# Layer 0 of a four-layer graph network: row steps ordered behind the value checks, constants made in steps over the first loads, six checks moved to layer 2

## The chip, the cores and the metric

The kernel runs on one core of a Trainium2 chip. The metric is device time in microseconds. The engines named below are PE (matrix multiplication), DVE (VectorE), ACT (ScalarE), POOL (GpSimd) and SP, whose queue issues the large loads from HBM.

## The reference

`x` is 4096 rows of 64 features, `adj` a 4096 x 4096 matrix of zeros and ones in float32 (64 MiB). Four layers follow each other, each `x = layernorm(x + layer(x, adj))`. All four read the whole of `adj`.

```python
# layer 0
deg = jnp.clip(jnp.sum(adj, axis=1, keepdims=True) + 1.0, 1.0, None)
h_neigh = (adj @ X + X) / deg
z = jnp.concatenate([X, h_neigh], axis=1) @ W + b
out = jax.nn.relu(z)
out = out / jnp.maximum(jnp.linalg.norm(out, axis=1, keepdims=True), 1e-12)
# layers 1 and 3: hyperbolic attention over the edges
adj_att = sigmoid(left[:, None] + right[None, :] + b_att) * adj
support_t = einsum('ij,ijd->id', adj_att, logmap(x[:, None], x[None, :], c))
out = proj(expmap(x, support_t, c), c)
# layer 2: the last 100 neighbours, weights halving with each step back
w = mask * where(pos > 0, 0.5 ** (k - pos), 0.0)
out = w @ (x @ weight) + bias
```

## The kernel before

`adj` is transposed on its way in and read four times, once in each layer. A layer works through four **groups** of 1024 output rows. `GROUPS` holds them in the order s = 3, 2, 1, 0; the text numbers them in the order of work, group 0 (s = 3) to group 3 (s = 0). Each group goes through 16 **loads** `g` = 15 down to 0. A load is one tile `edges`, 128 partitions by two blocks of 1024 columns in float32, 1.0486 MB, issued on SP's queue (L708). There are six buffers for such tiles; a buffer comes free when all that reads the tile is done.

In **layer 0** each load is used by eight matmuls (L1561, 128x512 each), which add up `adj @ X` in three bfloat16 parts together with the degree. Some loads are also used by a **check** (L871): a DVE instruction over the whole tile that counts the values other than 0 and 1, since the fast path assumes them. A check is done once for each of the 64 tiles of `adj` in the whole run: `checked_later(s, g)` says whether it is done in layer 0 or put off to layer 2, which reads the same tiles again. Before the change, eight loads of each group are checked in layer 0 (g = 4, 6, 8, 10 and 12 to 15) and eight in layer 2.

The **row work** of a group (the end of a layer for its 1024 rows, and the preparation of the next layer) is written as generators. `later` puts one into a queue. `tick` is called four times for each load in layer 0; it advances a place counter and runs the generators that are due, so a generator's `yield n` means "go on n ticks later", and its instructions are emitted between those of the loads. `mark` separates the instructions emitted by loads ("pairs") from those emitted by row steps. Where `anchored[0]` is set, it gives every row instruction on PE, ACT and DVE an order dependence on the last pair instruction of the same engine that was emitted ahead of it. Before the change `anchored[0]` is set only in the attention layers.

In layer 0 and layer 2, PE and ACT execute in the order of emission (`tc.manual_schedule(engines=FIXED)`). DVE and POOL do not: there a planner orders the instructions by its own estimate of when their inputs are ready, within the dependences.

The row work of a group in layer 0 is `end_0` (it starts in the first tick of the next group, with the matmuls L1510 and L1511), then `norm_rows` and `prepare`. `prepare` puts its second half, `second`, into the queue 44 ticks later: DVE's L975 to L1008, among them L994, L997 and L987, three copies on ACT (L971 to L973), small copies on POOL (L979 to L984), four sets of transposes on PE (L1023) with ACT's copies after them (L1027), and the attention scores. `linear` makes `x @ W` of the group's own rows (PE L1370 and L1381, DVE L1496). `constants` spreads the small parameters over the partitions (L1472, copied out at L1473), derives the curvature values (`curved`) and turns the two attention vectors into columns (`att_columns`, products at L855). The products and the spreading share one PSUM tile, `aux`.

`move` ends an attention layer for one group. Group 3's `move` of layer 1 and `supports`, which turns its rows into layer 2's operand, run inside layer 2's first pass, `wide_pass`, which works on groups 0 and 1 together (matmuls L1743 and L1755). There ACT's L1302 (tanh) and L1394 (the rows in half precision) stand at fixed places between the exponentials L1750.

Of the kernel before, what the change touches and what calls it, by code (L numbers as in the profile page):

```python
# [21 lines left out]
D = 64  # L22
# [39 lines left out]
def gnn_stack_kernel(  # L62
# [509 lines left out]
    def stream(fits):  # L572

        with ExitStack() as st:
# [57 lines left out]
            def later(steps, second=False, wait=0):  # L632
                queues[int(second)].append([steps, place[1] + wait])

            def in_turn(tag, *parts):
                for part in parts:
                    yield from (part or ())
                done.add(tag)
# [47 lines left out]
            def spare_ends():  # L686
                while held:
                    tick(1)
                spare.clear()
# [21 lines left out]

            def checked_later(s, g):

                return g in (0, 1, 2, 3, 5, 7, 9, 11)

            def grp(name, bufs=None):
                kw = {"bufs": bufs} if bufs else {}
# [129 lines left out]
                nc.scalar.dma_start(t, src[:, :, None, :].to_broadcast([1, 2, 2, D]))  # L847
                return t

            def att_columns(rows_of, name):  # L850


                t = aux.tile([P, 2], F32, name="aux")
                for u in range(2):
                    nc.tensor.matmul(  # L855
                        t[:, u : u + 1], rows_of[:, u].rearrange("p k d -> p (k d)"),
                        one_row[:, :1], start=True, stop=True,
                    )
                w = row.tile([P, 2], F32, name="att_w")
                V.tensor_copy(w, t)  # L860
                parts = keep.tile([P, 7], BF16, name=name)
                for k in range(3):
                    of = parts[:, k : k + 4 : 3]
                    V.tensor_copy(of, w)
                    V.tensor_sub(w, w, of)
                V.memset(parts[:, 6:], 1.0)
                return parts
# [7 lines left out]
            def curved(c, name, least):  # L875


                c2, sc, rsc, of_y, root, short, by_root, by_short = (
                    num(keep, name + n, 1)
                    for n in (  # L880
                        "_c2", "_sc", "_rsc", "_of_y", "_root", "_short", "_by_root", "_by_short",
                    )
                )
                V.tensor_scalar(c2, c, -2.0, None, ALU.mult)
                V.tensor_copy(rsc, rsqrt(c, "rsc"))
                V.tensor_mul(root, rsc, c)
                V.tensor_copy(by_root, rsc)
                V.tensor_scalar(by_short, rsc, 1.0 / least, None, ALU.mult)
                V.tensor_scalar(of_y, rsc, -((2.0 * UNIT) ** -0.5), None, ALU.mult)
                V.tensor_scalar(rsc, rsc, 0.996, None, ALU.mult)  # L890
                V.tensor_scalar(sc, root, -((2.0 * UNIT) ** 0.5), None, ALU.mult)
                V.tensor_scalar(short, root, least, None, ALU.mult)
                return c, c2, sc, rsc, of_y, root, short, by_root, by_short
# [551 lines left out]
            with ExitStack() as lp:  # L1445
# [23 lines left out]
                def constants():  # L1469

                    t = aux.tile([P, 2 * D + 3], F32, name="aux")
                    nc.tensor.matmul(t, one_row, given, start=True, stop=True)  # L1472
                    V.tensor_copy(given_b, t)  # L1473
                    V.tensor_mul(c1, r_sb, r_sb)
                    V.reciprocal(c1, c1)
                    V.memset(c3, 1.0)
                    V.tensor_copy(ident16, ident)
                    V.memset(sum_w[:, D:], 0.0)
                    V.tensor_copy(sum_w[D:, :D], w0_sb[D:, :])
                    V.memset(count_w, 0.0)  # L1480
                    V.memset(count_w[D:, D:], 1.0)
                    V.tensor_copy(count_w[:D, :D], sum_w[:D, :D])
                    return (
                        curved(c1, "k1", 1e-15**0.5), curved(c3, "k3", 1e-15),
                        att_columns(att_rows1, "att1"), att_columns(att_rows3, "att3"),
                    )

                V.memset(third[:, :, D : D + 1], 1.0)
                parts_of(GROUPS[0])
# [8 lines left out]
                def end_0(s, tops):  # L1498
# [43 lines left out]
                        1, s, att1, batt1_sb, curve1, 1e-15, good[:, 0], 70  # L1542
                    )

                with tc.manual_schedule(engines=FIXED):
                    for s in GROUPS:
                        sums = [ps.tile([P, W], F32, name="acc") for _ in range(2)]
                        counts = [ps.tile([P, W], F32, name="acc") for _ in range(2)]
                        parts = ((first, sums, P), (third, counts, D + 1))
                        for g in reversed(range(NB // 2)):  # L1550
# [22 lines left out]
                                                start=False, stop=False,  # L1573
                                            )
                            if s == GROUPS[0] and g == NB // 2 - 3:
                                curve1, curve3, att1, att3 = constants()
                                nc.scalar.dma_start(w2_sb, w2)
                                nc.scalar.dma_start(w2_twice[:D], w2)
                                nc.scalar.dma_start(w2_twice[D:], w2)
                                later(in_turn((0, s), linear(0, s, w0_sb[:D, :], own_part)))  # L1580
                            tick(4)
                        need((0, s))
                        tops = []
                        for h in range(2):
                            top = row.tile([P, W], F32, name="sums", bufs=2)
# [13 lines left out]
                            later(in_turn((0, s - 1), own_of))  # L1599

                spare_ends()


            place[0] = 1
# [285 lines left out]
```

## Time and profile before

| | us |
|---|---|
| median of three runs | 1066.32 (1062.9 to 1067.3) |
| the profiled execution's own time | 1064.98 |
| its span, first to last instruction | 1063.3 |
| PE busy | 985.4 (93%) |
| DVE busy | 901.2 (85%) |
| ACT busy | 753.4 (71%) |
| POOL busy | 339.1 (32%) |
| bytes moved | 271.62 MB, mean 255 GB/s |

Layer 0's matmuls run from 7.2 to 183 us of the span, layer 1's from 186 to 518, layer 2's first pass from 514 to 610. A busy PE is not PE at its peak, since matmuls are pipelined and their ends are modelled. In the lists of instructions the columns are start, duration, engine, line, operation, output from input, shapes and count, and in brackets the idle time of the engine ahead of it with what ended it. In the groups the columns are the count, busy time and mean duration in nanoseconds, and the idle time ahead. A wait of the DMA queue (SPq) names the engine and line that freed the buffer, with total time, count and longest.

### The profile page before, as it was taken

The page shows a single profiled execution, that of the slowest core. Times are in us where ns is not written, and L with a number is a line of the kernel's source. Part 1 is how long each engine was busy: PE and PEld are TensorE (multiplying, and loading weights), DVE is VectorE, ACT ScalarE, POOL GpSimd, SP SyncE. Part 2 cuts the span into 40 slices and gives each one's busy share as a digit, 9 for nine tenths or more (in the row PEclk, how much of TensorE's full clock was granted, in tenths as well). Part 3 has the DMA queues.
Part 4 walks back from the last instruction along what each step waited for, and adds up shares of the span by engine and source line. Part 5 has one row for each costly group of instructions (what it writes and reads, how often), then busy time and mean ns, then how long its engine had stood idle before and what let it go on. Part 6 is the DMA issues. An engine that isn't in the chain of part 4 may idle for free.

```text
span 1063.3 us, 13594 instructions
## 1 busy us (share of the span) xinstructions
PE 985.4 (93%) x4845; PEld 400.7 (38%) x4845; DVE 901.2 (85%) x1383; ACT 753.4 (71%) x876; POOL 339.1 (32%) x695
## 2 busy tenths in 40 slices
PE   4998998879999999999999999997999999999991
PEld 2454554323333333333333344442333333333330
DVE  6677878779999999999485579857899999999996
ACT  0013122859989888888677688896998888888970
POOL 0011222470064464455200020105401562573670
PEclk8999999989999999999999999998999999999996
DMA  8999999836665656566599999994465766665600
GB/s 338 369 420 367 389 390 387 336 107 222 216 220 198 238 204 232 198 224 219 218 331 341 372 357 314 322 328 179 163 240 194 245 226 209 237 218 198 228 3 22
DMA packets 38580, 271.62 MB, mean 255 GB/s; under 512 B 4710, under 2 KB 4710, under 8 KB 5734
## 3 DMA queue, kind: packets, MB, share of 16 engines
q1 hardware_dynamic: 37728, 270.03, 69.7%
q8 instruction: 40, 0.66, 0.2%
q10 hardware_dynamic: 774, 0.63, 0.2%
q14 instruction: 38, 0.31, 0.1%
HBM read 269.58 MB, written 1.05 MB: 255 GB/s over the span
## 4 chain that ended last, share of the span: by engine, by line
PE 66%; DVE 18%; POOL 5%; DMA 4%; ACT 4%; issue 2%; ACTq 0%; SPq 0%; POOLq 0%; DVEq 0%
PE acc L1121 18%; PE z L1743 11%; PE z L1143 8%; PE z L1149 8%; PE z L1146 7%; DVE t L1170 5%; DVE t L1167 5%; PE acc L1561 4%; DMA edges<-in_adj_dram 3%; PE z L1755 3%; DVE junk L871 2%; PE z L1709 2%; ACT sq L1750 1%; ACT sq L1164 1%; POOL sq L1525 1%
## 5 line engine op out<-in xcount | busy, mean ns | idle before, releaser
L1167 DVE SCALAR_TENSOR_TENSOR t<-z,sig 128x1024 f32<-128x1024 f32 x256 | 309.1, 1218 | 22.4 <-ACT sq L1164 19.8
L1164 ACT ACTIVATE sq<-z 128x1024 f32<-128x1024 f32 x256 | 255.4, 1022 | 62.1 <-PE z L1149 31.7
L1170 DVE SCALAR_TENSOR_TENSOR t<-sq,t 128x2048 f32<-128x2048 f32 x127 | 293.4, 2311 | 0.3
L1161 ACT ACTIVATE sig<-left_b,right 128x1024 f32<-128x1024 f32 x256 | 287.3, 1150 | 6.5 <-DVE t L1167 6.0
L1121 PE MATMUL acc<-t,xe 128*64 128x512 f32 x1024 | 261.5, 616 | 13.4 <-DVE t L1170 13.4
L1143 PE MATMUL z<-edges,two_i 128*128 128x512 bf16 x512 | 200.3, 391 | 6.2 <-DVE t L1167 6.2
L1149 PE MATMUL z<-dst,src 74*128 74x512 f16 x512 | 194.8, 380 | 0.0
L1146 PE MATMUL z<-lo_hi,hi_lo 128*128 128x512 f16 x512 | 193.7, 378 | 0.0
L1750 ACT ACTIVATE sq<-z 128x512 bf16<-128x512 f32 (+1 forms) x192 | 137.9, 741 | 39.5 <-PE z L1743 38.8
L1121 PEld LDWEIGHTS acc<-t,xe 128*64 128x64 f32 x1024 | 64.9, 138 | 144.4 <-issue 110.0
L871 DVE SCALAR_TENSOR_TENSOR t<-edges 128x2048 bf16<-128x2048 f32 x32 | 74.4, 2335 | 28.7 <-DMA edges<-in_adj_dram 28.6
L1561 PE MATMUL acc<-edges,first 128*128 128x512 bf16 x256 | 81.1, 398 | 18.1 <-DMA edges<-in_adj_dram 17.9
L1143 PEld LDWEIGHTS <-two_i 128*128 128x128 bf16 x512 | 50.3, 98 | 118.7 <-issue 73.1
L1743 PE MATMUL z<-edges,pass_by 128*128 128x512 bf16 x248 | 86.4, 388 | 6.3 <-ACT sq L1750 5.8
L1743 PE MATMUL z<-edges,enter 128*128 128x512 bf16 x256 | 88.2, 387 | 0.0
L871 DVE SCALAR_TENSOR_TENSOR junk<-edges 128x2048 bf16<-128x2048 f32 x32 | 73.1, 2284 | 14.9 <-DMA edges<-in_adj_dram 14.9
L1561 PE MATMUL acc<-edges,third 128*65 128x512 bf16 x256 | 80.5, 396 | 0.0
L1149 PEld LDWEIGHTS <-src 74*128 74x128 f16 x512 | 49.1, 96 | 73.5 <-issue 11.9
L1146 PEld LDWEIGHTS <-hi_lo 128*128 128x128 f16 x512 | 50.2, 98 | 63.7 <-issue 18.3
L1270 POOL TENSOR_TENSOR w_att<-x,u 128x512 f32<-128x512 f32 x6 | 18.2, 3028 | 169.9 <-ACT u L1264 169.9
L1709 PE MATMUL z<-sq,halves 128*128 128x512 bf16 x128 | 48.1, 377 | 0.6 <-ACT sq L1750 0.6
L1525 POOL TENSOR_TENSOR sq<-z 128x512 f32<-128x512 f32 x4 | 10.1, 2526 | 117.2 <-DVE z L1523 97.4
(466 smaller groups left out, 996.5 us busy)
## 6 DMA issues: line engine op xcount, KB each, us to landing
edges<-in_adj_dram SPq DMA_DIRECT2D x256, 1024.0 KB, 4.9
x<-in_x_dram SPq DMA_DIRECT2D x4, 256.0 KB
out_dram<-x ACTq DMA_DIRECT2D x2, 256.0 KB
out_dram<-x SPq DMA_DIRECT2D x2, 256.0 KB
w_sb<-in_L_gnn_W_dram ACTq DMA_DIRECT2D x1, 32.0 KB, 4.9
w_twice<-in_L_gnn_weight_dram ACTq DMA_DIRECT2D x2, 16.0 KB, 8.7
given<-in_L_gnn_b_dram ACTq DMA_DIRECT2D x1, 0.2 KB
given<-in_L_gnn_bias_dram ACTq DMA_DIRECT2D x1, 0.2 KB
```

Of the source, the lines that this page charges most:

```text
L871: V.scalar_tensor_tensor(junk, a, 0.0, a, ALU.not_equal, ALU.not_equal, accum_out=odd[:, n : n + 1])
L1121: it = nc.tensor.matmul(acc[h * D : (h + 1) * D, :], xe[:, j, :], t[:, k, h * W : (h + 1) * W], start=j == BLOCKS[0], stop=j == BLOCKS[-1],)
L1143: nc.tensor.matmul(half, two_i, edge[:, at : at + W], start=True, stop=False)
L1146: nc.tensor.matmul(half, hi_lo[:, of], lo_hi[:, to], start=False, stop=False)
L1149: last = nc.tensor.matmul(half, src[:, of], dst[:, to], start=False, stop=True)
L1161: nc.scalar.activation(sig, left_b, AF.Sigmoid, bias=right[:, j : j + 1])
L1164: nc.scalar.activation(sq[:, k], zp, AF.Square, bias=ROOT + OFF, scale=-1.0 / UNIT)
L1167: V.scalar_tensor_tensor(ts[k][:, k], zp, 0.0, sig, ALU.max, ALU.mult)
L1170: V.scalar_tensor_tensor(t, sq, HIGH**2, t, ALU.add, ALU.mult)
L1561: nc.tensor.matmul(accs[h][:m], lhs[:, j, :], edge[:, at : at + W], start=j == BLOCKS[0], stop=j == BLOCKS[-1],)
L1743: nc.tensor.matmul(z[:, h : h + W], lhs, rhs[:, h : h + W], start=j == BLOCKS[0], stop=True, skip_group_check=True,)
L1750: weighed[0] = nc.scalar.activation(w, z[:, :n], AF.Exp, bias=-(OFF_EDGE + CUT) * LN2, scale=-LN2)
```

## The change

- `checked_later`: in group 0 all loads with g under 12 are checked in layer 2; in group 1 also g = 4 and 6.
- `att_columns` is split: the products become `att_products`.
- `constants` becomes a generator with pauses of 4, 8, 8, 8 and 4 ticks, run in the queue ahead of the group's `linear`, where it had been emitted whole behind load g = 13. Its results are taken from the list `made` at the end of the group.
- `anchored[0]` is set in layer 0 for every group but the first, and cleared behind `spare_ends()`.

```diff
             def checked_later(s, g):

-                return g in (0, 1, 2, 3, 5, 7, 9, 11)
+                if s == GROUPS[0]:
+                    return g < 12
+                return g in (0, 1, 2, 3, 5, 7, 9, 11) or (s == GROUPS[1] and g in (4, 6))
...
-            def att_columns(rows_of, name):
-
+            def att_products(rows_of):
 
                 t = aux.tile([P, 2], F32, name="aux")
...
+                return t
+
+            def att_columns(t, name):
+
                 w = row.tile([P, 2], F32, name="att_w")
...
                     nc.tensor.matmul(t, one_row, given, start=True, stop=True)
+                    yield 4
                     V.tensor_copy(given_b, t)
+                    yield 8
                     V.tensor_mul(c1, r_sb, r_sb)
...
-                    return (
-                        curved(c1, "k1", 1e-15**0.5), curved(c3, "k3", 1e-15),
-                        att_columns(att_rows1, "att1"), att_columns(att_rows3, "att3"),
-                    )
+                    made.append(curved(c1, "k1", 1e-15**0.5))
+                    made.append(curved(c3, "k3", 1e-15))
+                    for rows_of, name in ((att_rows1, "att1"), (att_rows3, "att3")):
+                        w = att_products(rows_of)
+                        yield 8
+                        made.append(att_columns(w, name))
+                    yield 4
...
                     for s in GROUPS:
+                        anchored[0] = s != GROUPS[0]
...
                             if s == GROUPS[0] and g == NB // 2 - 3:
-                                curve1, curve3, att1, att3 = constants()
                                 nc.scalar.dma_start(w2_sb, w2)
                                 nc.scalar.dma_start(w2_twice[:D], w2)
                                 nc.scalar.dma_start(w2_twice[D:], w2)
-                                later(in_turn((0, s), linear(0, s, w0_sb[:D, :], own_part)))
+                                own_of = linear(0, s, w0_sb[:D, :], own_part)
+                                later(in_turn((0, s), constants(), own_of))
                             tick(4)
                         need((0, s))
+                        curve1, curve3, att1, att3 = made
...
                 spare_ends()
+                anchored[0] = False
```

## The prediction

> **What bounds the kernel now.** The change sits in layer 0 and in the first pass of layer 2, so I read those two stretches and not the shares of the whole span. First the page's groups: what one load of 128x2048 edge values costs on each engine.
>
> ```profile
> L871 DVE SCALAR_TENSOR_TENSOR junk<-edges 128x2048 bf16<-128x2048 f32 x32 | 73.1, 2284 | 14.9 <-DMA edges<-in_adj_dram 14.9
> L1561 PE MATMUL acc<-edges,first 128*128 128x512 bf16 x256 | 81.1, 398 | 18.1 <-DMA edges<-in_adj_dram 17.9
> ```
>
> A check costs VectorE 2.28 us. In the chain of waits, PE takes 1.8 us for the eight matmuls of a load. Then the DMA view of the first 230 us (slices of 5.75 us):
>
> ```profile
> GB/s 205 278 408 410 422 259 372 388 416 429 425 416 425 413 311 309 390 429 416 422 419 396 298 292 409 423 423 420 420 409 298 403 407 427 389 215 261 151 218 54
> ```
>
> Six slices in a row (46 to 80 us) average 421 GB/s: a load of 1.0486 MB then takes 2.49 us, more than PE's 1.8. So transfer is the floor, and the holes are the dips near 30, 83, 130 and 175 us. Table by stage:
>
> ```profile
> 17.00:31.00 14.00, 8.16 (x41) 5.03 (x39) 12.07 (x50) 0.58 (x1) 0.00 (x0) 0.65 0.97 396
> 57.20:99.60 42.40, 38.74 (x225) 21.72 (x224) 33.30 (x85) 7.79 (x12) 8.82 (x9) 1.00 0.96 385
> 99.60:143.50 43.90, 41.31 (x242) 23.51 (x241) 34.59 (x99) 10.55 (x17) 8.74 (x9) 0.96 0.96 383
> ```
>
> The first row holds the start, the others are groups 1 and 2 (counted in order of work from 0). Last columns: granted clock, DMA share, GB/s. The share says 0.96, the bytes say 383 of 421. Who holds the loads back is in the DMA queue's own waits, here for 0 to 47 us (first line) and 91 to 135 us (the other two):
>
> ```profile
> SPq L708 <- PE acc L1561: 19.3, 8, 7.5
> ...
> SPq L708 <- DVE junk L871: 31.1, 8, 6.0
> SPq L708 <- PE acc L1561: 5.5, 4, 2.7
> ```
>
> Early it is PE's matmuls, later the checks. PE's timeline has the early cause:
>
> ```profile
> 18.18 0.49 PE L1472 MATMUL aux<-given,one_row 1*128 1x131 f32 x2
> 23.71 1.01 PE L855 MATMUL aux<-one_row,xw 1*128 1x1 f32 x4 [5.04 <-DVE given_b L1473]
> ...
> 27.35 1.06 PE L1561 MATMUL acc<-edges,first 128*128 128x512 bf16 x2
> ```
>
> PE stands from 18.7 to 27.35 us in the constants: their products reuse one PSUM bank, which VectorE empties only at 23.4, behind two checks. Load g=12 had landed before 21.2 (its check ran then). The six edge buffers fill; no load is issued from 22 to 31 us. The later cause is in VectorE's timeline of group 2:
>
> ```profile
> 129.58 0.64 DVE L994 TENSOR_TENSOR xw<-x,g 128x512 f32<-128x512 f32 x1
> ...
> 131.32 0.68 DVE L997 TENSOR_TENSOR xe<-xw,m 128x512 f32<-128x512 f32 x1
> 131.92 2.29 DVE L871 SCALAR_TENSOR_TENSOR junk<-edges 128x2048 bf16<-128x2048 f32 x1
> ...
> 134.13 0.69 DVE L987 TENSOR_TENSOR ys<-y,ys 128x512 f16<-128x512 f32 x1
> ...
> 136.58 2.28 DVE L871 SCALAR_TENSOR_TENSOR junk<-edges 128x2048 bf16<-128x2048 f32 x1
> ```
>
> The two checks are g=6 and g=4. L994, L997 and L987 belong to `second`, which the program emits 44 steps (11 loads) after `prepare`, behind check g=4; the scheduler hoisted them.
>
> **What the Trainium skill says.** "VectorE: DVE Perf Modes", the perf-mode tier table: a two-input fp32 operation has only the 1x rate; for N=2048 it gives 2293 ns. The trace has 2284 ns, so a check can't be cheapened, only moved. "DMA: Bandwidth & Descriptors", Bandwidth: 425 GB/s for a 16 MB transfer; the 421 sustained here agrees. "Perfetto Trace Analysis", Identifying the Most-Contended Engine: occupancy of the 16 DMA engines misleads, use bytes; here 0.96 busy beside 383 GB/s agrees. "TensorE: Matmul & The Clock Gate", Part 1: after an idle window of about 3.4 us PE falls to half clock; after the 5 us wait the table has 0.65, and the next eight matmuls took 3.41 us instead of 1.81.
>
> **The change, part by part.** Six checks leave layer 0: g=4, 6, 8, 10 of group 0, g=4 and 6 of group 1; 6 x 2.28 = 13.7 us of VectorE go to layer 2. The instructions of the constants stay the same; PE gets them at g=13, g=10 and g=8, after which group 0's own linear part ends at g=0 instead of g=8. From group 1 on each row step on VectorE gets an order dependence on the last check emitted ahead of it; PE and ACT were in program order already.
>
> *Transfer floor.* By 28.75 us 9.91 MB were moved, 1.05 of it x: 8.45 loads. From there at 2.49 us each, load n lands at 28.75 + (n-8.45) x 2.49: load 17 at 50.0, 33 at 89.9, 64 at 167.1.
>
> *Group 0.* Without the stall PE takes g=12 at 18.7. Loads g=7 and g=6 are then released by their buffers' checks (ends 21.1 and 23.4, where they are now), the rest by PE alone. Transfer stays full. The copy to `given_b` (23.4) is there before PE reaches g=10's products (24.5): no new wait. PE ends load 17 at 50.0 + 1.8 = 51.8; before 57.2: **-5.4**.
>
> *Group 1.* Checks g=6 and 4 are gone. Check g=8 ended at 83.5; I shift it by the 5.4 to 78.1. Load 30 reuses its buffer and lands 4.9 us later (the page's median), 83.0 against a floor of 82.4: 0.6 lost. Load 33 lands at 90.5, PE ends it at 92.3; before 99.6: **-7.3**.
>
> *Group 2.* Check g=8 now ends at 127.4 - 7.3 = 120.1; load 46 lands at 125.0, against 122.9: 2.1 lost. Check g=6 loses the pieces of `second` hoisted ahead of it, 1.8 us (the small ones, L994 and L997): 134.2 - 7.3 - 1.8 = 125.1; load 48 lands at 130.0, where it is anyway. Load 49 at 132.5, done at 134.3; before 143.5: **-9.2**.
>
> *Group 3.* Check g=8 at 159.8, g=6 at 176.2 - 9.2 - 2.4 = 164.6; loads 62 and 64 could land at 164.7 and 169.5, the floor from 132.5 has 164.9 and 169.9. PE's last matmul ends near 172.2 (0.5 for the transposes ahead of it); before 183.0: **-10.8**. At the pure floor it would be -13.6.
>
> *The new wait.* `second` now stands behind check g=4. Behind it on VectorE is only the next group's check; PE's transposes L1023 wait for its L987, and load g=0's matmuls queue behind them. POOL's small copies of `second` (4.7 us, ended at 135.4 and 176.8) move along; only the third and fourth transposes need them, 6 us later in PE's order, and POOL is otherwise empty there. The three weight DMAs on ACT's queue stay at g=13. In group 2 check g=4 would end at 127.4, L987 some 3 us on at 130.4; PE arrives at 129.3, and load 48 lands at 130.0: 0 to 1 us, inside the 10.8, of which I keep **10.5**. After layer 0 comes a chain of POOL row steps and layer 1's pairs, bound by PE and VectorE (DMA share 0.62 from 290 to 515): the gain passes through.
>
> *Layer 2.* PE runs without a gap from 518 to 610 us, so only a delay that reaches PE counts. Checks don't hold loads there: load g=5 landed at 568.1 and PE releases it at 580.8, while its checks took until 573.2. What they can delay is the row chain of the last `move`, through ACT's fixed order:
>
> ```profile
> 542.14 0.23 DVE L1296 TENSOR_SCALAR un<-un,k_short 128x8 f32<-128x8 f32 x1
> ...
> 545.50 0.20 ACT L1302 ACTIVATE th<-un 128x8 f32<-128x8 f32 x1
> ...
> 560.72 0.69 DVE L1360 TENSOR_TENSOR x<-z,y 128x512 f32<-128x512 f32 x1
> ...
> 567.07 0.61 ACT L1394 CAST x_hl<-x 128x512 f16<-128x512 f32 x1
> ```
>
> The slack is 3.1 us ahead of L1302 and 5.7 ahead of L1394. Checks g=10 and g=8 (one each) fall into the chain: 2.3 and 4.6 us, within both. The pairs at g=6 and g=4 fit VectorE's gaps at 563.6 (4.5 us) and 573.2 (6.5 us in two). If check g=6 comes ahead of L1360 or a check waits for its load in front of the chain, some us come through. Bounds 0 and 9: if the whole chain stood behind the checks of g=6 (landed near 562, done at 566.7), its last 9 us would end near 576 instead of before 567. I take **1**. A gain is excluded: PE is full.
>
> Sum: -10.5 + 1 = -9.5. The profiled execution has a span of 1063.3 and a time of 1065.0; the median shown is 1066.3, 1.3 above. 1065.0 - 9.5 + 1.3 = 1056.8, say **1057**.
>
> **The rivals.**
> *Only the stall counts.* Order on VectorE may yield nothing: the norm steps, which legitimately follow check g=15, delay checks as before. For: most of the row work ahead of check g=8 is of that kind. Against: the hoisted pieces are seen. The early dips (slices 6 and 7) hold (421-259 + 421-372) x 5.75 / 421 = 2.9 us, and the missing checks of group 1 some 3: -3 to -6, 1060 to 1063.
> *The transposes become the wait (slower).* Place: L1023 behind L987 behind check g=4, in groups 2 and 3. Point: my 130.4 against PE's 129.3 and the load's 130.0, so it decides as soon as check g=4 is over 1 us later than I put it. Price: each further us once per group; with check g=4 ending where it ended and the 5 us of hoisted steps plus a check behind it, 7 us each: -7.3 + 14 = +6.7, 1073. For: the margin is thin. Against: the check itself moves up by the same pieces.
> *Layer 2 takes it back.* The chain behind all checks to g=6: +9 - 10.5 = -1.5, 1065.
> *It doesn't do what it says.* The scheduler may have other orders at the same cost, transfer stays at 385 GB/s: 1066.
>
> **Numbers.** About 0.5% (5.3 us) is what a measurement of this kernel can tell from no change. Forecast 0.62 (1052 to 1062), stall only 0.16 (half of it faster by over 0.5%), transposes 0.11, layer 2 0.06, nothing 0.05. Faster 0.70, same 0.18, slower 0.12. The range 1051 to 1064 leaves out the slower rival and the upper end of the last two.
>
> **What would show it.** PE with no wait over 1 us between 18 and 28 us and a clock of 1.0 there; GB/s near 421 from 12 to 80 us; group 1 begun near 52 us; VectorE with L994, L997 and L987 after check g=4 in groups 2 and 3; layer 0's last matmul near 172. In layer 2 PE without gaps, L1394 not waiting. A PE wait at L1023 over 2 us, or PE waiting on ACT near 545 or 567, would prove me wrong, as would layer 0 ending after 178.

## The result, and the profile after

| | us |
|---|---|
| before, median of 13 runs | 1066.32 |
| after, median of 13 runs | 1062.86 (1059.22 to 1070.47) |
| ratio after to before | 0.9965, 95% interval 0.9946 to 0.9984 |
| the profiled execution of after | 1065.97, span 1064.2 |

The change is worth 3.5 us; 9.5 were forecast. Executions of one kernel lie over 10 us apart, and the profiled one of after is 3.1 above its median, so what two profiles differ in is only taken for the change here where further profiles show it too.

Layer 0 first: the table by stage of after, with the start and groups 1 and 2 as in the prediction (the last three columns are granted clock, DMA share and GB/s), and then the DMA view of the first 230 us.

```profile
17.00:31.00 14.00, 10.50 (x52) 4.97 (x51) 12.65 (x55) 0.00 (x0) 0.00 (x0) 0.88 1.00 402
55.46:97.40 41.94, 38.29 (x221) 21.73 (x224) 29.08 (x76) 7.77 (x12) 6.75 (x9) 1.00 0.99 400
97.40:139.20 41.80, 39.32 (x237) 22.72 (x240) 35.33 (x99) 10.44 (x18) 6.75 (x9) 1.00 0.98 393
```

```profile
GB/s 195 302 400 373 427 416 423 416 427 417 422 417 426 373 315 423 420 425 413 427 390 311 349 427 426 423 415 416 355 388 426 426 376 262 219 214 164 241 187 0
```

The start moves 402 GB/s where it moved 396, with PE at clock 0.88 for 0.65; the hole near 30 us (259 before) is gone. The holes near 83, 123 and 165 us are still there. PE's timeline at the start:

```profile
17.86 0.49 PE L1477 MATMUL aux<-given,one_row 1*128 1x131 f32 x2
18.28 0.62 PE L1573 MATMUL acc<-edges,first 128*128 128x512 bf16 x2
...
25.65 1.01 PE L1573 MATMUL acc<-edges,first 128*128 128x512 bf16 x2 [3.25 <-DMA edges<-in_adj_dram]
```

The stall in the constants (L1477 is the old L1472) is gone, but PE now waits for a load, and falls to half clock again (1.01 us for a pair of matmuls, 0.61 at full clock). In the later groups the order on VectorE is as written: `second` (L992, L999, L1002) stands behind check g = 4 of group 2.

```profile
128.81 2.29 DVE L876 SCALAR_TENSOR_TENSOR junk<-edges 128x2048 bf16<-128x2048 f32 x1
...
131.10 0.68 DVE L992 TENSOR_TENSOR ys<-y,ys 128x512 f16<-128x512 f32 x1
132.06 0.68 DVE L999 TENSOR_TENSOR xw<-x,g 128x512 f32<-128x512 f32 x1
132.78 0.69 DVE L1002 TENSOR_TENSOR xe<-xw,m 128x512 f32<-128x512 f32 x1
```

Layer 0's end comes 4.4 us earlier ("deg 3" in the table of the experiments). Then two things eat it. The first is PE's clock at the handover to layer 1 (before: 1.00 all through):

```profile
178.00:182.00 4.00, 2.73 (x24) 2.31 (x22) 1.01 (x4) 3.98 (x7) 0.00 (x0) 1.00 1.01 422
182.00:186.00 4.00, 4.00 (x18) 2.95 (x18) 0.09 (x1) 3.15 (x4) 0.00 (x0) 0.58 1.02 426
186.00:190.00 4.00, 3.77 (x20) 2.66 (x21) 2.50 (x5) 0.36 (x1) 0.16 (x1) 0.57 0.97 360
```

The second is in layer 2's first pass. There the last group's rows `x` (VectorE, L1365) are split into two half-precision parts `x_hl`: a cast on ACT (L1399), then a subtraction on POOL (L1400), then PE's transposes (L1405). VectorE's timeline of after, and then ACT's, POOL's and PE's:

```profile
566.38 0.69 DVE L1365 TENSOR_TENSOR x<-z,y 128x512 f32<-128x512 f32 x1
566.98 2.28 DVE L876 SCALAR_TENSOR_TENSOR t<-edges 128x2048 bf16<-128x2048 f32 x1
...
569.19 3.23 DVE L876 SCALAR_TENSOR_TENSOR t<-edges 128x2048 bf16<-128x2048 f32 x1
```

```profile
567.15 0.62 ACT L1399 CAST x_hl<-x 128x512 f16<-128x512 f32 x1 [1.95 <-DVE x L1365]
```

```profile
567.84 2.43 POOL L1400 TENSOR_TENSOR x_hl<-x,x_hl 128x512 f16<-128x512 f32 x1 [25.37 <-ACT x_hl L1399]
```

```profile
570.33 0.62 PE L1405 MATMUL aux<-ident,x_hl 128*128 128x128 f16 x8 [3.36 <-POOL x_hl L1400]
```

The same place in before, POOL and VectorE:

```profile
543.30 1.16 POOL L1395 TENSOR_TENSOR x_hl<-x,x_hl 128x512 f16<-128x512 f32 x1 [30.22 <-ACT x_hl L1394]
567.76 1.16 POOL L1395 TENSOR_TENSOR x_hl<-x,x_hl 128x512 f16<-128x512 f32 x1 [23.30 <-ACT x_hl L1394]
```

```profile
543.35 3.26 DVE L871 SCALAR_TENSOR_TENSOR t<-edges 128x2048 bf16<-128x2048 f32 x1 [0.84 <-DMA edges<-in_adj_dram]
...
568.15 2.91 DVE L871 SCALAR_TENSOR_TENSOR t<-edges 128x2048 bf16<-128x2048 f32 x1 [4.54 <-DMA edges<-in_adj_dram]
```

Two things are to be read. First, in after ACT waits 1.95 us for `x`, and PE 3.36 us behind it; before, neither waited. Second, durations: POOL's subtraction takes 1.16 us or 2.43, a check 2.28 or 3.26. The one that is under way runs on at its usual pace; the other stands until it is done, which shows as a long instruction and not as a wait. In before POOL started 0.05 us ahead of the check at 543 and 0.39 ahead at 568; in after a check was already running. A check has two inputs in SBUF (the same tile twice). The Trainium skill, "SBUF — State Buffer", Who interferes with whom, states that a VectorE instruction with two SBUF inputs contends with a GpSimd instruction that reads SBUF, and that the order of issue decides which of the two is blocked. The durations agree (543.30 + 1.16 is 1.1 after the check's start, which is 0.98 longer than usual). The prediction priced the check on VectorE alone and not whom it locks out.

### The profile page after: what moved, and what is told of

It is laid out like the page before. It is cut to its first block, busy times and chain, and to the rows that moved or that the text cites. A ratio compares the mean times of both kernels' runs of the same rounds, so it can differ in the third digit from the quotient of the medians.

```text
span 1064.2 us, 13506 instructions
## 1 busy us (share of the span) xinstructions
PE 979.2 (92%) x4760; PEld 400.3 (38%) x4845; DVE 904.9 (85%) x1383; ACT 753.0 (71%) x876; POOL 327.6 (31%) x695
## 4 chain that ended last, share of the span: by engine, by line
PE 58%; DVE 23%; DMA 7%; POOL 4%; ACT 4%; issue 3%; ACTq 0%; SPq 0%; POOLq 0%; DVEq 0%
PE acc L1126 17%; PE z L1757 8%; PE z L1151 8%; PE z L1148 7%; PE z L1154 7%; DVE t L1172 6%; DVE t L1175 6%; DMA edges<-in_adj_dram 6%; DVE junk L876 3%; PE acc L1573 3%; PE z L1723 2%; PE z L1769 2%; ACT sq L1169 1%; ACT sq L1764 1%; DVE t L876 1%
## 5 line engine op out<-in xcount | busy, mean ns | idle before, releaser
L1148 PE MATMUL z<-edges,two_i 128*128 128x512 bf16 x463 | 182.7, 395 | 5.4 <-DVE t L1172 5.4
L876 DVE SCALAR_TENSOR_TENSOR t<-edges 128x2048 bf16<-128x2048 f32 x38 | 87.3, 2310 | 20.9 <-DMA edges<-in_adj_dram 20.7
L1573 PE MATMUL acc<-edges,first 128*128 128x512 bf16 x241 | 77.0, 396 | 21.9 <-DMA edges<-in_adj_dram 21.2
L1757 PE MATMUL z<-edges,enter 128*128 128x512 bf16 x248 | 85.9, 387 | 0.4
L876 DVE SCALAR_TENSOR_TENSOR junk<-edges 128x2048 bf16<-128x2048 f32 x26 | 59.4, 2285 | 11.7 <-DMA edges<-in_adj_dram 11.6
L1723 PE MATMUL z<-sq,halves 128*128 128x512 bf16 x122 | 45.9, 377 | 0.8 <-ACT sq L1764 0.6
L1380 ACT COPY x_t<-aux 64x512 f32<-64x512 f32 x8 | 4.6, 576 | 58.3 <-PE aux L1375 58.3
```

The source lines that it names most:

```text
L876: V.scalar_tensor_tensor(junk, a, 0.0, a, ALU.not_equal, ALU.not_equal, accum_out=odd[:, n : n + 1])
L1148: nc.tensor.matmul(half, two_i, edge[:, at : at + W], start=True, stop=False)
L1573: nc.tensor.matmul(accs[h][:m], lhs[:, j, :], edge[:, at : at + W], start=j == BLOCKS[0], stop=j == BLOCKS[-1],)
L1757: nc.tensor.matmul(z[:, h : h + W], lhs, rhs[:, h : h + W], start=j == BLOCKS[0], stop=True, skip_group_check=True,)
```

## The experiments

All profiles in one table. "deg" is the start of the first reciprocal in each group's end (L1516 before, L1526 after), 1.93 us behind PE's first matmul of that end in groups 0 to 2, 2.0 to 2.3 in group 3. "Gap" is the time from group 3's first to its second reciprocal: 4.06 at PE's full clock. "Pass" is layer 2's first pass, between the copies of the sums that end layer 1 and the pass. The subtractions are POOL's first and second `x_hl` in layer 2 (v: on VectorE). Ratios are to before, with 95% interval.

| kernel | deg 0 | deg 1 | deg 2 | deg 3 | gap | pass | subtractions | ratio |
|---|---|---|---|---|---|---|---|---|
| before | 59.14 | 101.53 | 145.40 | 185.41 | 4.06 | 92.94 | 1.16, 1.16 | |
| after | 57.39 | 99.36 | 141.14 | 180.99 | 6.13 | 96.27 | 1.15, 2.43 | 0.9965 (0.9946 to 0.9984) |
| e1 after again | 56.29 | 97.00 | 139.00 | 179.57 | 6.42 | 97.23 | 1.15, 2.43 | 0.9964 (0.9949 to 0.9979) |
| e2 checks alone | 59.75 | 101.61 | 144.93 | 184.97 | 4.07 | 97.22 | 1.15, 2.42 | 1.0024 (1.0007 to 1.0041) |
| e3 constants alone | 55.78 | 98.21 | 141.74 | 185.53 | 5.71 | 96.34 | 3.18, 1.16 | 0.9989 (0.9969 to 1.0009) |
| e4 order alone | 59.43 | 100.74 | 141.61 | 181.45 | 6.93 | 96.35 | 3.19, 1.15 | 0.9979 (0.9959 to 0.9999) |
| e5 constants, order | 56.05 | 96.79 | 137.62 | 177.44 | 4.07 | 96.36 | 3.20, 1.15 | 0.9941 (0.9923 to 0.9959) |
| e10 the same again | 56.66 | 97.35 | 138.30 | 178.16 | 6.93 | 92.93 | 1.16, 1.16 | 0.9952 (0.9931 to 0.9973) |
| e13 e5, group 0's checks moved | 56.81 | 97.99 | 142.50 | 182.34 | 6.29 | 98.04 | 1.15, 2.43 | 0.9968 (0.9953 to 0.9982) |
| e9 e5, group 1's checks moved | 56.95 | 97.51 | 138.49 | 178.34 | 4.06 | 92.93 | 1.16, 1.16 | 0.9901 (0.9874 to 0.9928) |
| e14 the same again | 57.27 | 98.04 | 139.84 | 181.39 | 4.06 | 96.41 | 3.24, 1.16 | 0.9948 (0.9929 to 0.9967) |
| e8 no checks in layer 0 | 54.85 | 95.57 | 135.35 | 174.75 | 6.22 | 97.22 | 1.16, 2.43 | 0.9942 (0.9922 to 0.9961) |
| e6 after, rows on VectorE | 57.38 | 97.93 | 142.30 | 182.13 | 6.93 | 96.04 | v, v | 0.9965 (0.9949 to 0.9981) |
| e7 late checks, rows on VectorE | 57.05 | 97.78 | 138.83 | 178.65 | 4.06 | 92.32 | v, v | 0.9941 (0.9921 to 0.9962) |
| e11 before, first rows on VectorE | 58.93 | 101.36 | 144.96 | 185.60 | 4.07 | 92.51 | v, 1.15 | 0.9971 (0.9954 to 0.9988) |
| e12 e5, first rows on VectorE | 56.69 | 97.42 | 139.93 | 179.77 | 4.07 | 92.51 | v, 1.15 | 0.9923 (0.9894 to 0.9951) |
| e15 e9, first rows on VectorE | 55.54 | 96.27 | 138.02 | 177.86 | 6.36 | 92.52 | v, 1.16 | 0.9935 (0.9905 to 0.9964) |

### The parts, each alone

**e1**, the changed kernel unedited.

> The changed kernel, nothing edited, for a second profile. Theory: layer 0 gains 5.3 us (last matmul near 177.7), but PE had stood for about a microsecond before the last group's row steps and falls to half clock from 182 to 190 us, so that layer 1 starts only 1.3 to 2 us earlier than before; in layer 2's first pass the row chain stands behind the extra checks and the pass loses 3.3 us. Median near 1062.9, ratio near 0.9965, and the profile repeats both. Rival: the half clock belongs to the one execution that was profiled; then this profile has full clock from 182 to 190, layer 1's group sums come 4 to 5 us earlier than before (near 283), and the layer 2 pass ends 1 to 2 us earlier than before, near 609.

Half clock (gap 6.42) and the long subtraction come again, the pass loses 4.3 us (3.3 expected), and the ratio is the same: the rival falls. But layer 0's groups scatter by 1 to 2 us between two profiles of one program: group 1 took 41.97 us in the first and 40.71 in this one.

**e2**, the moved checks alone.

```diff
-                return g in (0, 1, 2, 3, 5, 7, 9, 11)
+                if s == GROUPS[0]:
+                    return g < 12
+                return g in (0, 1, 2, 3, 5, 7, 9, 11) or (s == GROUPS[1] and g in (4, 6))
```

> The kernel before with the six moved checks alone. Theory (the checks cost more in layer 2 than they free in layer 0): PE's stall at 18.7 to 27 us stays, group 0 still ends near 57; group 1 ends 0 to 3 us earlier; layer 2's first pass loses about 3 us. Sum -1 to +3, ratio 0.999 to 1.003. Rival (transfer in layer 0 is the floor and layer 2 hides them): group 1 gains 2 to 3 us and it stays, layer 2 costs 1 or less: -2, ratio 0.998.

Slower by 0.24%: layer 0 gains 0.4 us, the pass loses 4.3. As expected, at its upper end; the rival falls.

**e3**, the constants in steps alone (the `constants` and `att_products` part of the change's diff).

> The kernel before with the constants made in steps alone, all checks where they were, row steps not bound. Theory (several loads in flight land late, so taking the stall away gives only what the loads had landed for): group 0 ends at 55 to 56 in place of 57.2, groups 1 to 3 keep this 1.5 to 2 us, half of it is left in layer 1: -1 to -2, ratio 0.998 to 0.999. Rival (my forecast's sum): group 0 ends at 52 and -5 stays in the end: ratio 0.995.

Group 0's end comes 3.4 us earlier, more than the 1.2 to 2.2 expected and less than the rival's 5. Some 1.2 us of it (an estimate, 0.5 MB at 421 GB/s) are a better start of this execution and not the edit: 3.5 MB had been moved by 11.5 us (3.4 and 3.5 in e8 and e15), 2.8 to 3.0 in all other profiles. Group 3 loses it again in this profile: PE waited 2.24 us for a load at 177.5 and went to half clock. The ratio is the one expected, but its interval holds 1.

**e4**, the order alone.

```diff
                     for s in GROUPS:
+                        anchored[0] = s != GROUPS[0]
...
                 spare_ends()
+                anchored[0] = False
```

> The kernel before with the row steps of groups 1 to 3 bound behind the checks alone. Theory: in groups 2 and 3 the pieces of the second half of prepare no longer run ahead of the last two checks, which gives 2 us in group 2 and 1 to 2 in group 3; layer 0 ends 3 to 4 us earlier, of which 1 to 3 reach layer 1: ratio 0.997 to 0.999. Rival (the order is worth nothing, the loads are held by checks g=10 and g=8 behind the norm steps): groups 2 and 3 keep their 43.9 and 39.5 us, ratio 1.000. Second rival: the transposes behind the bound steps become PE's wait, +3 or more.

Group 2 takes 40.87 us from deg to deg in place of 43.87, and group 1 1.1 less; group 3 gains 0.2 where 1 to 2 were expected. That is 4 us at the end of layer 0, as expected, 2.9 of them lost in the gap. No wait of PE at the transposes of `second`: that rival falls here as in after.

The three ratios add up to about -0.1%. The whole change gives -0.35%. The checks may interact with the rest, or parts lost something by chance: each ratio's interval is 0.17 to 0.2% to either side.

### Which checks take it back

**e5**, constants and order, no check moved.

```diff
-                if s == GROUPS[0]:
-                    return g < 12
-                return g in (0, 1, 2, 3, 5, 7, 9, 11) or (s == GROUPS[1] and g in (4, 6))
+                return g in (0, 1, 2, 3, 5, 7, 9, 11)
```

> The changed kernel with the checks left where they were before: constants in steps and bound row steps only. Theory: layer 0 ends 4 to 6 us earlier than before, as in the changed kernel, since the moved checks freed loads that nothing waited for; PE's half clock at 182 to 190 us keeps 1 to 3 us of it; in layer 2's first pass it is open which of a check on VectorE and the subtraction x_hl on POOL starts first near 543 us (if the check does, POOL's takes 3.2 instead of 1.16 us and the pass loses 3). Median 1062 to 1064, ratio 0.996 to 0.998, no better and no worse than the changed kernel. Rival (the moved checks cost 3 us in layer 2 and give nothing): 1060, ratio 0.994. Second rival (the moved checks carry layer 0's gain): layer 0 ends at 181 or later and the ratio is 0.999.

The first rival holds: 1059.7 us. Layer 0 ends 8 us earlier than before, with full clock at the handover. My theory had the moved checks as neutral. The profile still shows the first subtraction blocked. The interval overlaps that of after; what the further runs say together follows e14.

**e10**, the same kernel once more.

> Constants in steps and bound row steps alone once more, for a second profile and more times. Theory (the half clock of PE at the handover comes or not by the moment at which the execution meets it, whatever the kernel; the first subtraction x_hl is blocked by a check nearly always): layer 0 ends near 174 again, POOL's subtraction near 535 takes 3.2 us again, the clock between 174 and 188 may be full or half; median 1059 to 1061, ratio 0.9935 to 0.995. Rival (half clock belongs to the changed kernel's order): full clock again, layer 1's first group sums near 279.

Both accidents changed sides: now the clock is half and the first subtraction free. The ratio, 0.9952, is just above the 0.9935 to 0.995 expected. Tables of e5 (the first) and of e10, in stretches of 3.41 us, the step in which each profile's clock changes (the part on the prediction comes back to it); the clock stands third from the end:

```profile
176.40:179.81 3.41, 2.58 (x18) 1.82 (x18) 1.03 (x3) 3.38 (x4) 0.00 (x0) 1.00 1.01 425
179.81:183.22 3.41, 3.34 (x29) 2.50 (x29) 1.64 (x4) 2.16 (x3) 0.00 (x0) 1.00 1.02 425
```

```profile
175.19:178.60 3.41, 2.71 (x25) 2.26 (x22) 0.45 (x3) 3.39 (x7) 0.00 (x0) 1.00 1.01 425
178.60:182.01 3.41, 3.06 (x9) 1.59 (x10) 0.63 (x2) 2.02 (x2) 0.00 (x0) 0.50 1.03 430
182.01:185.42 3.41, 3.18 (x16) 3.13 (x16) 0.29 (x2) 2.06 (x2) 0.00 (x0) 0.50 1.01 423
185.42:188.84 3.42, 3.42 (x15) 1.77 (x15) 2.21 (x4) 0.34 (x1) 1.03 (x1) 0.50 0.61 187
```

PE was busy 2.58 and 2.71 us of the first stretch, and the one with more went to half clock. POOL's timelines of the two say the same of the subtraction (e5 first):

```profile
534.88 3.20 POOL L1398 TENSOR_TENSOR x_hl<-x,x_hl 128x512 f16<-128x512 f32 x1 [30.22 <-ACT x_hl L1397]
```

```profile
540.22 1.16 POOL L1398 TENSOR_TENSOR x_hl<-x,x_hl 128x512 f16<-128x512 f32 x1 [30.22 <-ACT x_hl L1397]
```

In e5 the check, which had waited for its load, started at 534.77, 0.11 us ahead of POOL. My expectation that this happens nearly always was wrong; among the kernels whose group 0 checks are not moved and whose first rows are on POOL it happened in four of seven profiles.

**e13**, e5 with group 0's four checks moved.

```diff
+                if s == GROUPS[0]:
+                    return g < 12
                 return g in (0, 1, 2, 3, 5, 7, 9, 11)
```

> Constants in steps, bound row steps, and of the moved checks group 0's four alone (g = 4, 6, 8 and 10). Theory (they are the loss: with them VectorE goes from check to check between 557 and 575 us, so that POOL's second subtraction always meets one): POOL takes 2.4 us near 560 to 567, PE waits about 3 us at the transposes, layer 2's first pass takes 96 to 97 us; layer 0 is no faster than without the move; ratio 0.996 to 0.998. Rival (the loss needs all six checks): ratio 0.994 to 0.9955, the second subtraction 1.16 us.

As expected: the subtraction takes 2.43 us, PE waits 3.5 us, and the ratio is that of after; the pass takes 98.04, more than the 96 to 97 expected. VectorE's timeline shows why the second subtraction has no chance; it started on POOL at 570.08:

```profile
568.61 0.69 DVE L1365 TENSOR_TENSOR x<-z,y 128x512 f32<-128x512 f32 x1
569.22 2.28 DVE L876 SCALAR_TENSOR_TENSOR t<-edges 128x2048 bf16<-128x2048 f32 x1
...
571.43 3.23 DVE L876 SCALAR_TENSOR_TENSOR t<-edges 128x2048 bf16<-128x2048 f32 x1
```

Checks stand one behind the other. Between the end of `x` and the end of ACT's cast the planner has a check ready, whose load is there already.

**e9**, e5 with group 1's two checks moved.

```diff
-                return g in (0, 1, 2, 3, 5, 7, 9, 11)
+                return g in (0, 1, 2, 3, 5, 7, 9, 11) or (s == GROUPS[1] and g in (4, 6))
```

> The changed kernel with group 0's four checks left in layer 0: of the six moved checks only g = 4 and 6 of group 1 go to layer 2. Theory: moving six costs some 2.5 us (checks alone 1.0024, and 0.9964 with them against 0.9941 without), most of it by the checks of group 1 that fall beside the second subtraction x_hl at 567 us: POOL then takes 2.4 us in place of 1.16 and PE waits 2 to 3 us; ratio to before 0.995 to 0.9965. Rival (group 0's g = 10, 8 and 6 make VectorE's queue full; without them the second subtraction is free): PE's wait at 567 under 0.5 us, ratio 0.994.

The rival holds: the second subtraction is free, and 1057.0 us is the best median of all.

**e14**, the same once more.

> Constants in steps, bound row steps and group 1's two checks moved, once more. Theory (half clock and blocked first subtraction come by chance, some 3 us each; the second subtraction is free): layer 0 ends near 175, pass of 93 or 96.4 us, ratio 0.990 to 0.9935, median 1057 to 1060. Rival (the first six times were a lucky draw): 1061, ratio 0.995, like the version without moved checks.

Here its rival holds: 1061.4 us. The second subtraction is free again, the first was blocked. The first six times were a lucky draw; the two kernels with and without group 1's checks can't be told apart. The two runs are of one program, and their intervals (0.9874 to 0.9928 and 0.9929 to 0.9967) don't meet: an interval from six runs is to be read with care.

For group 0's move the runs say more together. With each time taken relative to the mean of before beside it, the 57 executions with group 0's checks moved (after, e1, e13) average 0.9969 and the 39 without (e5, e9, e10, e14) 0.9938, an estimate from the recorded times: some 3.3 us lie in that move, with a standard error of some 0.7.

So in all five profiles with group 0's four checks moved and the rows on ACT and POOL (after, e1, e2, e13, and e8 below) the second subtraction was blocked and the pass took 96 to 98 us; in none of the other ten with that subtraction on POOL was it blocked.

### The floor of layer 0

**e8**, the changed kernel without layer 0's checks.

```diff
+            V.memset(odd, 0.0)
...
-                            if not checked_later(s, g):
-                                check(s, g, a, own.tile([P, 2, WW], BF16, name="junk"))
```

> The changed kernel with the 26 checks of layer 0 left out (their counts are set to zero); layer 2's checks stay. It measures what transfer alone allows in layer 0. My forecast's floor (2.49 us a load from 28.75 us on): groups of 39.9 us, group 0 done at 51.8, the last matmul at 170 to 172. Theory now: group 0 ends at 54 to 55 all the same, since the loads in flight at the start land 3.5 us later than their bytes were counted; from there groups of 40 to 40.5 us, the last matmul at 174 to 176; it gains 2 to 4 us over the changed kernel up to there. Rival (checks don't hold the loads any more, PE and landing do): groups stay at 41.5 to 42 us, last matmul at 177 to 178.

It lies between my forecast and the second theory: group 0 is done at 52.9 (51.8 and 54 to 55), groups 1 and 2 take 40.7 and 39.8 (39.9 and 40 to 40.5), and the last matmul ends near 172.4 (the pure floor was 169.4; 174 to 176). The DMA view has no hole after 12 us:

```profile
GB/s 201 384 410 403 414 424 419 425 419 425 416 423 420 422 416 423 422 416 422 423 420 420 420 423 420 419 417 423 420 420 419 262 187 231 202 276 157 208 1 3
```

So the 4.8 and 6.2 us from here to e1 and after (deg 3) go with the 26 checks that stay in layer 0, apart from the 1.2 us of the better start. The DMA queue's own wait for checks in the first 227 us is 104.3 us before, 83.3 in after and none here. As a measure of the loss it doesn't serve: it is 104.9 in e5, whose layer 0 ends 3.5 us ahead of after's.

### Taking POOL's subtraction away

**e6**, after with both halves of `x_hl` on VectorE in layer 2.

```diff
-                nc.scalar.copy(hl[:, :, :D], xg)
-                nc.gpsimd.tensor_sub(hl[:, :, D:], xg, hl[:, :, :D])
+                (V.tensor_copy if place[0] == 2 else nc.scalar.copy)(hl[:, :, :D], xg)
+                (V if place[0] == 2 else nc.gpsimd).tensor_sub(hl[:, :, D:], xg, hl[:, :, :D])
```

> The changed kernel with both halves of x_hl in layer 2 made on VectorE, where the cast was on ACT and the subtraction on POOL. Theory (the pass loses its 3 us because POOL's subtraction stands still while a check runs on VectorE, 2.43 us for 1.16, and PE waits for it): the subtraction on VectorE takes under 0.8 us, but one check lies between cast and subtraction in VectorE's order, so PE's wait ahead of the transposes falls from 3.4 to some 1 to 3 us; pass shorter by 0.5 to 2 us, ratio to before 0.994 to 0.996. Rival (the chain's delay is VectorE's queue of checks alone, POOL is only the messenger): the wait stays at 3 us or over, ratio 0.9965.

PE's wait falls from 3.4 to 2.2 us as expected, the pass is only 0.2 to 1.2 shorter than in the two profiles of after, and the ratio doesn't move, where 0.994 to 0.996 was expected. The planner put one check between the cast and the subtraction: the same check delays the chain in VectorE's order that had delayed it through the ports.

**e7**, the same rows on VectorE with constants and order, and group 0's checks at g = 8 to 15 in layer 0 and below in layer 2.

```diff
+                if s == GROUPS[0]:
+                    return g < 8
                 return g in (0, 1, 2, 3, 5, 7, 9, 11)
```

> Constants in steps and bound row steps as in the changed kernel; of group 0 the loads with g under 8 are checked in layer 2, of the other groups the eight of before, and both halves of x_hl are made on VectorE in layer 2. No check stands between the rows x and the subtraction in VectorE's order. Theory: layer 0 ends 4 to 6 us earlier as in the changed kernel; layer 2's first pass has no PE wait over 0.5 us at the transposes of x_hl and takes 93 us, as in the profile of before, in place of 96 to 97; what is left after the half clock is 1.5 to 3 us from layer 0, and 1.5 to 3 us from layer 2, since the kernel before too loses its 3 us there in some executions: ratio 0.992 to 0.995, median 1058 to 1061. Rival (layer 2's loss has another place, or layer 0 is lost again): ratio 0.9965 or more.

As expected: no wait at the transposes, a pass of 92.3 us, 1059.7.

**e11**, before with both halves of group 2's rows on VectorE; **e12** the same on e5, **e15** on e9.

```diff
-                nc.scalar.copy(hl[:, :, :D], xg)
-                nc.gpsimd.tensor_sub(hl[:, :, D:], xg, hl[:, :, :D])
+                (V.tensor_copy if s == GROUPS[2] else nc.scalar.copy)(hl[:, :, :D], xg)
+                (V if s == GROUPS[2] else nc.gpsimd).tensor_sub(hl[:, :, D:], xg, hl[:, :, :D])
```

> The kernel before, with both halves of x_hl of group 2 (the first of the two subtractions in layer 2, near 543 us) made on VectorE; the second stays on ACT and POOL. Theory (in most executions of the kernel before a check starts a moment ahead of POOL's subtraction, which then takes 3.2 us and costs the pass 3.4; its profile was one of the few without): the first pass takes 92 to 93 us, as in that profile, and the times fall by 2 to 3 us: ratio 0.997 to 0.998. Rival (the profile of before shows its usual state): ratio 1.000.

As expected: this edit alone makes the kernel before 0.29% faster, nearly as much as the whole change. Its one profile had been an execution without the accident. The edit changes more than the engine, though: the planner put this cast and subtraction 30 us earlier (512.6 us in place of 542.6), with a check between them, where nothing waits for them.

> Constants in steps, bound row steps, all checks where they were before, and both halves of x_hl of group 2 made on VectorE. Theory: layer 0's 4 to 6 us and layer 2's 3.4 us add up: first pass of layer 2 92 to 93 us in place of 96.4, ratio 0.991 to 0.992, median 1056 to 1058, or 2 to 3 us under the same without the last edit. Rival (another wait takes the place of POOL's): ratio 0.994.

The pass takes 92.5 us, and the median is 1058.8: 2.7 us below e10, which ran beside it, 0.9923 where 0.991 to 0.992 was expected. Its interval, 0.9894 to 0.9951, meets those of after (0.9946 to 0.9984) and e1 (0.9949 to 0.9979) only at its end.

> Constants in steps, bound row steps, group 1's two checks moved, and both halves of x_hl of group 2 made on VectorE. Theory: no subtraction meets a check, the first pass of layer 2 takes 92 to 93 us in every execution, only the half clock at the handover is left to chance: ratio 0.989 to 0.992, median 1056 to 1058. Rival (the blocked first subtraction was rare with group 1's checks moved): the same as without this edit within 0.001.

The pass is 92.5 us again, the clock was half, and 0.9935 is outside the 0.989 to 0.992 expected; against e14 beside it (0.9948) the edit gives 1.4 us, within the intervals. e7, e12 and e15 lose least in layer 2 (92.3 to 92.5 us for the pass), and of e5, e7, e9, e10, e12, e14 and e15, all without group 0's move as the change has it, every one has a lower ratio than after.

## Why the prediction was wrong

| term of the sum | forecast | after | e1 |
|---|---|---|---|
| group 0 | -5.4 | -1.8 | -2.9 |
| group 1 | -1.9 | -0.4 | -1.7 |
| group 2 | -1.9 | -2.1 | -1.9 |
| group 3 | -1.3 | -0.2 | +0.6 |
| gap at the handover | 0 | +2.1 | +2.4 |
| rest of layer 1 | 0 | +0.4 | +0.6 |
| layer 2's first pass | +1 | +3.3 | +4.3 |

The measured columns are differences to the one profile of before, which had neither accident. Three steps of the prediction failed: layer 0 gained 4.4 and 5.8 us (deg 3) where 10.5 were forecast, most of it missing in group 0; the gain didn't pass the handover whole; and layer 2 cost 3.3 and 4.3 us where 1 was put. In sum the columns say +1.4 us at the end of the pass. The medians say -3.5. Other executions of before seem to lose 3 us in the pass (e11's gain suggests it; none was profiled), and not every execution of after can lose as much as the two profiled, which are among the slow ones (e1's is the slowest of 22).

- **What bounded it: right.** Transfer is the floor of layer 0, loads wait for buffers, and without checks transfer runs at 420 GB/s with no hole and comes within 1.1 us of the floor at group 0 and 3 at the end (e8, with its better start). The 2293 ns of the Trainium skill's table stand there for `tensor_tensor`; the check is a `scalar_tensor_tensor`, with 2284 measured. That it can't be cheapened was not tested.
- **Group 0: the size failed.** The stall is gone, and the transfer did stay full: the view of after has 421 GB/s from 28.75 to 51.75 us. The step that failed is "load n lands at 28.75 + (n-8.45) x 2.49", which takes bytes moved for loads landed. In after PE ended load 17 at 55.5 us, so it had it at 53.7; by then the DMA view has the bytes of 18.35 loads, since those behind it were under way at the same time. The 1.35 loads are 3.4 us, nearly all of the 3.6 that are missing. What shows is a new wait of PE for a load: 3.25 us in after, 2.05 in e1, and 1.84 even in e8, without any checks, where group 0 gains 4.3.
- **Group 1: the checks g = 4 and 6 were not what held it.** The step "checks g=6 and 4 are gone" credited 1.9 us; e2 has 0.5, and e5, where they stay, takes the same 40.7 from deg to deg as e1. The gain goes with the order: 1.1 in e4 alone, none in e3 without it. Without the two checks loads 30 to 34 go out within 3 us in after, and load 32 lands 11.0 us after its issue (4.8 in before): again several are under way together.
- **Group 2: right.** L992, L999 and L1002 follow check g = 4, and the group takes 41.8 us for the 42.0 forecast. In e6 and e13 it takes 44.4 and 44.5: PE waits 2 us for a load near 134 there and goes to half clock behind it.
- **Group 3: the size failed.** In after check g = 6 ended 30.9 us into the group (30.3 forecast), load and matmuls behind it took 7.8 (7.6), and PE then waited 0.4 for ACT's copy of the sums. Three small misses, but the whole gain was to be 1.3.
- **The transposes, the slower rival: did not come.** PE has no wait there in any profile.
- **"The gain passes through": failed.** It named the pairs of layer 1 as bound by PE and VectorE and left out PE's clock. Half clock of 7 to 10 us at the handover took 1.7 to 2.9 us in nine of seventeen profiles. The Trainium skill, "TensorE: Matmul & The Clock Gate", Part 1, has the clock set by a free-running window of about 3.4 us. The traces agree: in each profile all stretches at half clock up to 1030 us begin on one grid of 3.41 us and last one, two or three of its steps, and the grid lies differently in each execution. In the nine with half clock at the handover a step begins 1.8 to 3.3 us ahead of deg 3; of the eight without, only e2 has one there, and before, e5 and e11 have none. So it hangs for the most part on where the grid happens to lie, and one program shows both sides (e5, e10). The idle window of about 3.4 us, which the prediction took from the same page, was not needed: in the step ahead PE was busy 65 to 86% of the time by the profile, and no wait was over 0.83 us. Why such a step is enough stays open.
- **Layer 2: right place, failed price.** I took 1 us where the bounds were 0 and 9. The slack ahead of ACT's cast was put at 5.7 us and the delay at 4.6, two checks. Measured from the end of layer 1, `x` comes 7.6 us later than before, behind nine checks of this pass where it had been five: 1.9 over the slack, the 1.95 us that ACT waits. Check g = 6 of group 0 came ahead of the rows, as the prediction named among what would let some through. The 1.3 us on POOL were not foreseen, nor that PE loses clock behind the wait (0.83 from 565 to 575 us in e1): in nine of the ten passes in which PE waited 2 us or more, all but after's, one step of 3.41 us at half clock followed.
- **A gain in layer 2 was excluded, "PE is full".** True of the profile; not of other executions of before, as e11's gain of 2.8 us suggests.
- **What stays open:** with group 0's checks moved layer 0 also ends later, deg 3 at 181.3 in the mean of four profiles (after, e1, e6, e13) for 178.8 of seven without (e5, e7, e9, e10, e12, e14, e15). About half of it is group 2 of e6 and e13. Why fewer checks should be slower was not found; the two sets overlap, and it may be chance.

## What to carry to other kernels

Work that is moved from a stage where it holds transfers to one where its engine is half idle is not free: look at what runs there beside it, on which engines, with which ports, and how near it starts to the chain that sets the stage. A stretch of idle time on VectorE may be just what lets a short POOL instruction through; keep long VectorE instructions with two inputs away from it, or take the POOL instruction off the chain. And one profile is one draw: where a 3 us accident hangs on 0.1 us, look at two or three profiles of the kernel before, ahead of pricing anything.

## What had not been expected of the hardware

- A check (the same fp32 tile as both inputs, 128x2048) and POOL's subtraction of 128x512 met 26 times in the 17 profiles, and one of them always stood: POOL's took 2.42 to 3.24 us in place of 1.16 (nine times), or the check 2.68 to 3.26 in place of 2.28 (seventeen). No check was long without such a meeting. Starts 0.05 to 0.9 us apart decided which.
- The same happens in layer 0, before the change as after it: POOL's product `sq` in the norm steps (L1525 before, L1535 after) takes 1.04 us where no check runs, as in all groups of e8, and 2.95 to 3.29 where it starts within 0.25 us of one. In four profiles it stood though its start is recorded 0.1 us ahead of the check's, as here in after, where a short VectorE instruction runs at that moment; the two starts alone don't tell which will stand.

```profile
106.34 3.29 POOL L1535 TENSOR_TENSOR sq<-z 128x512 f32<-128x512 f32 x1 [19.81 <-DVE q L1047]
106.36 0.17 DVE L1059 SCALAR_TENSOR_TENSOR f<-q,tt 128x8 f32<-128x8 f32 x1
106.44 2.29 DVE L876 SCALAR_TENSOR_TENSOR junk<-edges 128x2048 bf16<-128x2048 f32 x1
```

- PE goes to half clock for 7 to 10 us though no wait ahead is over 0.83 us: busy 79% of the step of 3.41 us ahead (e10), and in the same place not at 76% (e5). All such stretches lie on a grid that differs from one execution to the next.
- With no check in layer 0, 420 GB/s was held from 12 to 178 us (e8); before, groups 1 and 2 averaged 385 and 383.
